# Layer 1's maxima turned one head at a time, in column order, and the softmax factors applied three steps later

## The chip, the cores and the metric

The kernel runs on one core of a Trainium2 chip. The metric is the device time of one execution in microseconds (us). Engines are named as the profile names them: PE multiplies matrices (PEld is its weight load), DVE is the vector engine, ACT the scalar engine, POOL the GpSimd engine, and SP issues most of the DMA. PE writes to PSUM, a memory of eight banks of 128 x 512 fp32 values; everything else lies in SBUF or in DRAM.

## The reference

Two attention layers follow each other on an image batch x of shape (2, 256, 64, 64), so 4096 positions for each of two batch elements. The first has heads of 16 channels and ends in a gated residual with a sigmoid. The change concerns the second:

```python
qkv = jnp.einsum('oc,bchw->bohw', w_qkv, x) + b_qkv[None, :, None, None]
qkv = qkv.reshape(b, HEADS, 3 * head_dim, h * w)          # 4 heads of 64
q, k, v = jnp.split(qkv, 3, axis=2)
attn = jax.nn.softmax(jnp.einsum('bhdn,bhdm->bhnm', q, k) * scale, axis=-1)
out = jnp.einsum('bhnm,bhdm->bhnd', attn, v).reshape(b, c, h, w)
return jnp.einsum('oc,bchw->bohw', w_out, out) + b_out[None, :, None, None] + x
```

Each row of the softmax runs over all 4096 keys. All of it is fp32.

## The kernel before, in words

Layer 1 is cut into 32 units (b, g, j): batch element, pair of heads, block of 512 queries. A unit goes over the 4096 keys in 32 chunks of 128. For one chunk, `score` (L847) makes the scores of both heads, 128 keys by 2 x 512 queries, in a PSUM tile of two banks called "pair", of which there are two. `keep` (L864) takes a running maximum of them on DVE (`rmax`, L875; the very first chunk of a unit needs none) and copies them to SBUF on ACT (`raw`, L876). The ring of raw tiles holds 26 chunks.

The softmax's maximum is taken in two groups of 16 chunks. When a group's scores are all made, `turn_max` (L882) transposes the running maxima with eight 128 x 128 transposes, both heads into one tile of the pair kind, so that keys lie along the free side; `fold` (L893) reduces them on DVE to one negated maximum for each query (L898), writes these to DRAM (`neg`, L902) and reads them back spread over all partitions (`row`, L904). `place_shift` (L917) copies that row to PSUM. Twenty-two chunks after its score, a chunk gets the row added on DVE (`shift`, L925), its exponential on ACT (`weigh`, L937), and is added to a sum over keys on POOL (`acc`, L947 and L949; the first chunk of a group needs no addition of its own). A chunk or two later `gather` multiplies it with the values (`av`, L959).

When all chunks of a unit are through, the totals over keys are made on PE (`total`, L989), copied (L997), written to DRAM by four small DMAs and read back with queries along the partitions (`sums`, L1001). `factors` (L1014) scales the first group's sums, adds the two groups' on POOL (L1019, L1020), takes the reciprocal on DVE (L1022) and one product on POOL (L1023). `turn_sums` (L1026) transposes the unit's output four times for each group into the one bank of the "misc" kind, `rows` (L1029) multiplies by the factor on DVE (L1033) and adds on POOL (L1040, L1044), and a DMA writes the attention rows to DRAM (L1050).

The order on each engine is written out by hand. The main loop goes in steps of two chunks, so a unit has 16 steps, and unit n+1's step 0 follows unit n's step 15; the shifts lag 11 steps behind the scores. A step issues, in this order: both scores, the exponential of the second chunk of the step before, "start" and "early" work, keep and shift and exponential of the first chunk, "early end" work, keep of the second chunk, two gathers, "late" and "late end" work, shift of the second chunk. The planned extra work hangs at such places by the calls of `at`. In steps as counted here, with a unit's own late work falling in the next unit: keys and values of a later pair of heads at steps 2, 3, 5 and 6, next queries at 10 and 11, a group's maxima at 0 and 8, the shift row at 3 and 11, totals at 12, factors at the start of 14, rows of both groups in step 14. All users of "misc" (keys, values, queries, totals, turned outputs, output projections) share its one bank. SP runs its DMAs in order, and one that has to wait keeps back those behind it.

At the end of the kernel, the output projection's first half is filled in between the last steps by a list of steps (`FILL`, `project_half` at L1167).

Of the kernel before, what the change touches and what calls it, by code (L numbers as in the profile page):

```python
# [26 lines left out]
def conv_attention_kernel(  # L27
# [19 lines left out]
    nc = tc.nc  # L47
    B, _, N = x.shape
    NJ = N // NB
    NM = N // P  # L50
    PB = NB // P
# [3 lines left out]
    small = ctx.enter_context(tc.tile_pool(name="small", bufs=2))  # L55
# [83 lines left out]
    ident = const.tile([P, P], F32, tag="ident", name="ident")  # L139
# [68 lines left out]
    seq = tc.keep_in_program_order  # L208
# [3 lines left out]
    def at(t, place, step):  # L212
        extras.setdefault((t, place), []).append(step)
# [19 lines left out]
    with own0:  # L233
# [322 lines left out]
        for n, u in enumerate(units0):  # L556
# [6 lines left out]
            if u == units0[-1]:  # L563
                t1 = t0 + NM + 9
# [5 lines left out]
            else:  # L570
                t1 = t0 + NM + 15
# [79 lines left out]
        def misc(name):  # L651
            return small_bank[0](name)
# [57 lines left out]
        for i in range(NJ):  # L710
            k = (0, 0, i)
            t1 = T0 + 2 + 2 * i
# [3 lines left out]
            t1 = T0 + 20 + 3 * i if i < PB else END0 + (2, 3, 4, 9)[i - PB]  # L716
# [42 lines left out]
    GS = NM // 2  # L759
    NG = NM // GS  # L760
    LAG = GS // 2 + 3
    US = NM // 2
    END = len(units) * US
# [3 lines left out]
    with (  # L767
# [11 lines left out]
        rts = {}  # L779
        outs = {}  # L780
        halves_of = {}
        kd, vd = (
# [8 lines left out]
        neg1 = {  # L791
            (u, n): dram.tile([2, NB], F32, tag=f"neg_{u}_{n}", name=f"neg_{u[0]}{u[1]}{u[2]}_{n}")
            for u in units for n in range(NG)
        }
        sum1 = {
            u: dram.tile([NG * 2, NB], F32, tag="sum_{}_{}_{}".format(*u), name=f"sum_{u}")
            for u in units
        }
# [76 lines left out]
                seq(nc.vector.tensor_tensor(rmax[u, n], ps, before, ALU.max))  # L875
            seq(nc.scalar.copy(raw, ps))  # L876

        def by_query(a, i):

            return a.rearrange("p (q i) -> p i q", i=PB)[:, i, :]  # L880

        def turn_max(u, n):  # L882

            b, g, j = u
            ps = psp.tile([P, 2, NB], F32, tag="pair", name=f"rt_{b}_{g}_{j}_{n}")
            for k in range(2):
                for i in range(PB):
                    seq(nc.tensor.transpose(  # L888
                        ps[:, k, bass.ts(i, P)], by_query(rmax[u, n][:, k, :], i), ident
                    ))  # L890
            rts[u] = ps

        def fold(u, n):  # L893


            b, g, j = u
            nm = small.tile([P, 2, PB], F32, tag="negs", bufs=2 * NG, name=f"negs_{b}_{g}_{j}_{n}")
            seq(nc.vector.tensor_reduce(  # L898
                nm, rts.pop(u).rearrange("p k (i m) -> p k i m", m=P), AX.X, ALU.max, negate=True,
            ))  # L900
            to = neg1[u, n]
            nc.sync.dma_start(out=to.rearrange("k (p i) -> p k i", i=PB), in_=nm)  # L902
            row = l1.tile([P, 2, NB], F32, tag="row", bufs=1, name=f"row_{b}_{g}_{j}_{n}")
            nc.sync.dma_start(  # L904
                out=row.rearrange("p k n -> p (k n)"),
                in_=to.rearrange("(o k) n -> o (k n)", o=1).partition_broadcast(P),
            )
            rows_in[u, n] = row
            negs[u, n] = nm
            if n == 1:  # L910

                lost = small.tile([P, 2, PB], F32, tag="lost", name=f"lost_{b}_{g}_{j}")
                seq(nc.gpsimd.tensor_tensor(lost, nm, negs.pop((u, 0)), ALU.subtract))
                negs.pop((u, 1))
                losts[u] = lost

        def place_shift(u, n):  # L917
            b, g, j = u
# [75 lines left out]
        def keep_total(u):  # L994
            b, g, j = u
            row = l1.tile([P, NB], F32, tag="kv", name=f"srow_{b}_{g}_{j}")
            seq(nc.scalar.copy(row, srows[u]))  # L997
            for m in range(2 * NG):
                nc.sync.dma_start(out=sum1[u][m : m + 1, :], in_=row[32 * m : 32 * m + 1, :])
            s = small.tile([P, NG, 2, PB], F32, tag="sums1", name=f"sums1_{b}_{g}_{j}")  # L1000
            nc.sync.dma_start(  # L1001
                out=s.rearrange("p n k i -> p (n k) i"),
                in_=sum1[u].rearrange("m (p i) -> p m i", i=PB),
            )
            srows[u] = s
            seq(nc.scalar.activation(losts[u], losts[u], AF.Exp, scale=D1**-0.5))

        def turned(a, name):
            ps = misc(name)
            for i in range(PB):  # L1010
                seq(nc.tensor.transpose(ps[:, bass.ts(i, P)], by_query(a, i), ident))  # L1011
            return ps.rearrange("p (i k d) -> p k i d", k=2, d=D1)

        def factors(u):  # L1014

            b, g, j = u
            s = srows.pop(u)
            lost = losts.pop(u)
            seq(nc.gpsimd.tensor_tensor(s[:, 0], s[:, 0], lost, ALU.mult))  # L1019
            seq(nc.gpsimd.tensor_tensor(s[:, 1], s[:, 1], s[:, 0], ALU.add))  # L1020
            f = small.tile([P, NG, 2, PB], F32, tag="f1", name=f"f1_{b}_{g}_{j}")
            seq(nc.vector.reciprocal(f[:, 1], s[:, 1]))  # L1022
            seq(nc.gpsimd.tensor_tensor(f[:, 0], f[:, 1], lost, ALU.mult))  # L1023
            joined[u] = f

        def turn_sums(u, n):  # L1026
            avs1[u, n] = turned(avs1[u, n], "turned_{}_{}_{}_{}".format(*u, n))

        def rows(u, n):  # L1029
            b, g, j = u  # L1030
            ps = avs1.pop((u, n))
            r = l1.tile([P, 2, PB, D1], F32, tag="rows", name=f"rows_{b}_{g}_{j}_{n}")
            seq(nc.vector.tensor_tensor(  # L1033
                r, ps, joined[u][:, n].unsqueeze(3).to_broadcast([P, 2, PB, D1]), ALU.mult
            ))
# [12 lines left out]
            for k in range(2):  # L1048
                queue = (nc.sync, nc.scalar)[k if last else 0]
                queue.dma_start(  # L1050
                    out=to[2 * g + k, bass.ts(j, NB), :].rearrange("(p i) d -> p i d", i=PB),
                    in_=r[:, k, :, :],
                )
                if last:
                    c = ((2 * g + k) * N + j * NB) // D1
                    queue.dma_start(
                        out=last_att[0][c % P : c % P + NB // D1, :],
                        in_=att[b][c : c + NB // D1, :],
                    )
# [29 lines left out]
        for n, u in enumerate(units):  # L1089
            b, g, j = u  # L1090
# [6 lines left out]
            if n < len(units) - NJ:  # L1097
                to = (*units[n + NJ][:2], j)
# [84 lines left out]
        for i in range(NJ - 3):  # L1183
# [96 lines left out]
```

## Time and profile before

| | |
|---|---|
| median of 3 executions | 4988.03 us (4970.19 to 4988.19) |
| the profiled execution | 4990.49 us, span of its profile 4988.7 us |
| PE busy over the span | 4573.0 us (92%) |
| DVE busy | 3908.3 us (78%) |
| ACT busy | 3427.6 us (69%) |
| POOL busy | 2499.0 us (50%) |
| layer 0, from the span's start to 2050 us | PE 2031.87, DVE 1440.72, ACT 1200.74, POOL 149.32 us busy |
| layer 1's main part, 2050 to 4900 us | PE 2478.00, DVE 2425.66, ACT 2203.70, POOL 2328.80 us busy |
| its end, 4900 to 4988.7 us | PE 63.11, DVE 41.92, ACT 23.17, POOL 20.88 us busy |

The two layers have different limits, so busy shares over the whole span say little. In layer 1 four engines work in a chain on two score tiles, and what a stage costs is read from its waits: the number in square brackets behind an instruction in the view by time is how long its engine stood idle before it, and what ended that.

### The profile page before, as it was taken

The page shows a single profiled execution, that of the slowest core. Times are in us where ns is not written, and L with a number is a line of the kernel's source. Part 1 is how long each engine was busy: PE and PEld are TensorE (multiplying, and loading weights), DVE is VectorE, ACT ScalarE, POOL GpSimd, SP SyncE. Part 2 cuts the span into 40 slices and gives each one's busy share as a digit, 9 for nine tenths or more (in the row PEclk, how much of TensorE's full clock was granted, in tenths as well). Part 3 has the DMA queues.
Part 4 walks back from the last instruction along what each step waited for, and adds up shares of the span by engine and source line. Part 5 has one row for each costly group of instructions (what it writes and reads, how often), then busy time and mean ns, then how long its engine had stood idle before and what let it go on. Part 6 is the DMA issues. An engine that isn't in the chain of part 4 may idle for free. (4 is left out here: it accounts for less than half of the span.)

```text
span 4988.7 us, 69799 instructions
## 1 busy us (share of the span) xinstructions
PE 4573.0 (92%) x26998; PEld 1533.3 (31%) x26998; DVE 3908.3 (78%) x4456; ACT 3427.6 (69%) x4508; POOL 2499.0 (50%) x1294
## 2 busy tenths in 40 slices
PE   8999999999999999888888888888889988888887
PEld 4433333333333333322222322222223222222222
DVE  6777777777777774488888888888888888888885
ACT  3366666666666666688777787878777777787773
POOL 5300000000000000188888888888877788888883
PEclk9999999999999999999999999999999999999998
DMA  3000000000000001211111110112112111000012
GB/s 98 32 6 18 18 18 14 23 14 14 14 16 14 14 12 46 68 31 38 30 37 52 49 33 30 37 30 64 43 55 69 59 47 55 24 20 24 22 32 77
DMA packets 132625, 174.65 MB, mean 35 GB/s; under 512 B 54584, under 2 KB 63608, under 8 KB 132164
## 3 DMA queue, kind: packets, MB, share of 16 engines
q1 hardware_dynamic: 130868, 169.59, 11.2%
q8 instruction: 212, 3.47, 0.3%
q14 instruction: 121, 0.99, 0.1%
q10 hardware_dynamic: 1424, 0.59, 0.1%
HBM read 127.66 MB, written 42.48 MB: 34 GB/s over the span
## 5 line engine op out<-in xcount | busy, mean ns | idle before, releaser
L949 POOL TENSOR_TENSOR acc<-acc,raw 128x1024 f32<-128x1024 f32 x883 | 2092.6, 2370 | 272.1 <-ACT raw L937 216.5
L402 DVE TENSOR_REDUCE mx<-a 128x1 f32<-128x512 f32 x2048 | 1315.3, 686 | 448.9 <-PE a L398 447.9
L439 ACT ACTIVATE p<-s 128x512 f32<-128x512 f32 x2048 | 1107.8, 595 | 702.1 <-PE a L398 369.3
L876 ACT COPY raw<-s 128x1024 f32<-128x1024 f32 x1024 | 1037.0, 1013 | 545.9 <-DVE rmax L875 451.8
L858 PE MATMUL s<-q,k 64*128 64x512 f32 x4096 | 1149.2, 654 | 192.2 <-ACT raw L876 188.5
L875 DVE TENSOR_TENSOR rmax<-s,rmax 128x1024 f32<-128x1024 f32 x960 | 1169.7, 1218 | 108.6 <-PE s L858 103.5
L925 DVE TENSOR_TENSOR raw<-raw,shift 128x1024 f32<-128x1024 f32 x1024 | 1236.5, 1211 | 20.3 <-ACT shift L920 19.5
L436 PE MATMUL s<-q,kT 32*128 32x512 f32 x4096 | 1217.8, 640 | 0.0
L937 ACT ACTIVATE raw<-raw 128x1024 f32<-128x1024 f32 x1024 | 1087.2, 1062 | 100.3 <-DVE raw L925 59.0
L398 PE MATMUL a<-kT,q 32*128 32x512 f32 x4096 | 1129.0, 643 | 1.4 <-DVE mx L402 1.3
L959 PE MATMUL av<-raw,v 128*64 128x512 f32 x4096 | 1021.8, 620 | 1.7 <-ACT avs L976 1.7
L451 PE MATMUL av<-p,v 128*32 128x256 f32 (+1 forms) x7904 | 650.1, 399 | 0.6 <-ACT avs L465 0.6
L858 PEld LDWEIGHTS s<-q,k 64*128 64x128 f32 x4096 | 333.0, 192 | 979.4 <-ACT raw L876 715.7
L436 PEld LDWEIGHTS s<-q,kT 32*128 32x128 f32 x4096 | 397.0, 183 | 425.9 <-issue 392.8
L501 POOL TENSOR_TENSOR f<-f,dyn 128x16 f32<-128x16 f32 x15 | 3.3, 221 | 1027.4 <-DVE f L500 1027.4
L959 PEld LDWEIGHTS av<-raw,v 128*64 128x64 f32 x4096 | 255.6, 140 | 627.5 <-issue 529.6
L451 PEld LDWEIGHTS av<-p,v 128*32 128x32 f32 x7904 | 157.6, 108 | 751.5 <-issue 737.3
L552 POOL TENSOR_SCALAR res<-res 128x1024 f32<-128x1024 f32 x16 | 16.7, 1045 | 660.0 <-ACT res L551 660.0
L398 PEld LDWEIGHTS a<-kT,q 32*128 32x128 f32 x4096 | 305.0, 183 | 31.5 <-DVE mx L402 18.2
L947 POOL TENSOR_TENSOR acc<-raw,raw 128x1024 f32<-128x1024 f32 x64 | 152.5, 2383 | 240.0 <-ACT raw L937 240.0
L898 DVE TENSOR_REDUCE negs<-rt 128x8 f32<-128x1024 f32 x64 | 78.4, 1224 | 131.5 <-PE rt L888 131.5
L1011 PE MATMUL turned<-ident,avs 128*128 128x128 f32 x256 | 59.6, 370 | 116.6 <-DVE rows L1033 116.6
(319 smaller groups left out, 1789.4 us busy)
## 6 DMA issues: line engine op xcount, KB each, us to landing
row<-neg SPq DMA_DIRECT2D x64, 512.0 KB
x<-in_x_dram SPq DMA_DIRECT2D x16, 512.0 KB
res<-in_x_dram SPq DMA_DIRECT2D x16, 512.0 KB
x<-res SPq DMA_DIRECT2D x16, 512.0 KB
att<-rows SPq DMA_DIRECT2D x63, 128.0 KB
kd<-k1s SPq DMA_DIRECT2D x24, 256.0 KB
vd<-v1s SPq DMA_DIRECT2D x24, 256.0 KB
k<-kd SPq DMA_DIRECT2D x24, 256.0 KB
```

The lines of the kernel that those rows point to most:

```text
L398: seq(nc.tensor.matmul(ps, qs0[u][r, bass.ts(i, P)], kTs[b][r, bass.ts(m, NB)], start=True, stop=True,))
L402: seq(nc.vector.tensor_reduce(mxs[u][:, i * H + h, m : m + 1], ps, AX.X, ALU.max))
L436: seq(nc.tensor.matmul(ps, kTs[b][r, bass.ts(m, P)], qs0[u][r, :], start=True, stop=True))
L439: seq(nc.scalar.activation(pt[:, k, :], ps, AF.Exp, scale=D0**-0.5))
L451: seq(nc.tensor.matmul(avs[u][32 * h : 32 * h + 32, cols], vs0[b][:, m, 32 * h : 32 * h + 32], pts[t, h // 2][:, h % 2, cols], start=(m == ...
L858: seq(nc.tensor.matmul(ps[:, k, :], ks[b, g, m // PB][r, bass.ts(m % PB, P)], qs1[u][r, :], start=True, stop=True,))
L875: seq(nc.vector.tensor_tensor(rmax[u, n], ps, before, ALU.max))
L876: seq(nc.scalar.copy(raw, ps))
L925: seq(nc.vector.tensor_tensor(raws[t], raws[t], shifts[u, t % NM // GS], ALU.add))
L937: seq(nc.scalar.activation(p, p, AF.Exp, scale=D1**-0.5))
L949: seq(nc.gpsimd.tensor_tensor(accs[u, n], accs[u, n], p, ALU.add))
L959: seq(nc.tensor.matmul(avs1[u, n][k * D1 : (k + 1) * D1, :], v[:, m % PB, k, :], raws[t][:, k, :], start=(m % GS == 0), stop=(m % GS == GS ...
```

## The change

It has four parts. First, `turn_max` and `fold` handle one head at a time: four transposes into the misc bank and a reduction of 512 elements, at the places "early" and "late" of the same step in which both heads were handled together; each head has its own DMA to DRAM and back. Second, the transposes take contiguous columns where they took every fourth (`by_query` is gone). With that, partition p holds queries p, p + 128, p + 256 and p + 384 in place of four neighbours, so the DMAs of maxima and sums move single fp32 values where they moved four, and the attention rows go out in pieces of 64 values where a partition wrote 256 in one piece. Third, the difference of the two groups' maxima (`lose`) gets its own place in step 9. Fourth, the two sums on POOL move from the start of step 14 to the end of step 13, the reciprocal and the product to the start of step 15, and the rows to step 17, which is step 1 of the unit after; the list of fills at the kernel's end moves with them.

```diff
-            ps = psp.tile([P, 2, NB], F32, tag="pair", name=f"rt_{b}_{g}_{j}_{n}")
-            for k in range(2):
-                for i in range(PB):
-                    seq(nc.tensor.transpose(
-                        ps[:, k, bass.ts(i, P)], by_query(rmax[u, n][:, k, :], i), ident
-                    ))
-            rts[u] = ps
+            ps = misc(f"rt_{b}_{g}_{j}_{n}_{k}")
+            for i in range(PB):
+                seq(nc.tensor.transpose(
+                    ps[:, bass.ts(i, P)], rmax[u, n][:, k, bass.ts(i, P)], ident
+                ))
+            rts[k] = ps
...
-                nm, rts.pop(u).rearrange("p k (i m) -> p k i m", m=P), AX.X, ALU.max, negate=True,
+                nm, rts[k].rearrange("p (i m) -> p i m", m=P), AX.X, ALU.max, negate=True
             ))
-            to = neg1[u, n]
-            nc.sync.dma_start(out=to.rearrange("k (p i) -> p k i", i=PB), in_=nm)
-            row = l1.tile([P, 2, NB], F32, tag="row", bufs=1, name=f"row_{b}_{g}_{j}_{n}")
-            nc.sync.dma_start(
-                out=row.rearrange("p k n -> p (k n)"),
-                in_=to.rearrange("(o k) n -> o (k n)", o=1).partition_broadcast(P),
-            )
+            nc.sync.dma_start(out=to.rearrange("o (i p) -> p (o i)", p=P), in_=nm)
+            nc.sync.dma_start(out=rows_in[u, n][:, k, :], in_=to.partition_broadcast(P))
+
+        def lose(u):
+
+            b, g, j = u
+            lost = small.tile([P, 2, PB], F32, tag="lost", name=f"lost_{b}_{g}_{j}")
+            seq(nc.gpsimd.tensor_tensor(lost, negs.pop((u, 1)), negs.pop((u, 0)), ALU.subtract))
+            losts[u] = lost
...
-                in_=sum1[u].rearrange("m (p i) -> p m i", i=PB),
+                in_=sum1[u].rearrange("m (i p) -> p m i", p=P),
...
-                seq(nc.tensor.transpose(ps[:, bass.ts(i, P)], by_query(a, i), ident))
+                seq(nc.tensor.transpose(ps[:, bass.ts(i, P)], a[:, bass.ts(i, P)], ident))
...
-        def factors(u):
-
-            b, g, j = u
-            s = srows.pop(u)
-            lost = losts.pop(u)
+        def add_sums(u):
+            s, lost = srows[u], losts[u]
             seq(nc.gpsimd.tensor_tensor(s[:, 0], s[:, 0], lost, ALU.mult))
             seq(nc.gpsimd.tensor_tensor(s[:, 1], s[:, 1], s[:, 0], ALU.add))
+
+        def factors(u):
+
+            b, g, j = u
             f = small.tile([P, NG, 2, PB], F32, tag="f1", name=f"f1_{b}_{g}_{j}")
-            seq(nc.vector.reciprocal(f[:, 1], s[:, 1]))
-            seq(nc.gpsimd.tensor_tensor(f[:, 0], f[:, 1], lost, ALU.mult))
+            seq(nc.vector.reciprocal(f[:, 1], srows.pop(u)[:, 1]))
+            seq(nc.gpsimd.tensor_tensor(f[:, 0], f[:, 1], losts.pop(u), ALU.mult))
             joined[u] = f
...
-                    out=to[2 * g + k, bass.ts(j, NB), :].rearrange("(p i) d -> p i d", i=PB),
+                    out=to[2 * g + k, bass.ts(j, NB), :].rearrange("(i q) d -> q i d", q=P),
...
-                at(t1, "early", lambda u=u, k=k: turn_max(u, k))
-                at(t1, "early end", lambda u=u, k=k: fold(u, k))
+                for i, place in enumerate(("early", "late")):
+                    at(t1, place, lambda u=u, k=k, i=i: turn_max(u, k, i))
+                    at(t1, f"{place} end", lambda u=u, k=k, i=i: fold(u, k, i))
...
-            at(t1 + 6, "start", lambda u=u: factors(u))
+            at(t1 + 1, "late", lambda u=u: lose(u))
+            at(t1 + 5, "late end", lambda u=u: add_sums(u))
+            at(t1 + 7, "start", lambda u=u: factors(u))
             for place, k in (("early", 1), ("late", 0)):
-                at(t1 + 6, place, lambda u=u, k=k: turn_sums(u, k))
-                at(t1 + 6, f"{place} end", lambda u=u, k=k: rows(u, k))
+                at(t1 + 9, place, lambda u=u, k=k: turn_sums(u, k))
+                at(t1 + 9, f"{place} end", lambda u=u, k=k: rows(u, k))
...
-            (END + GS // 2 + 4, "early end"): (3,), (END + GS // 2 + 5, "early"): (4,),
-            (END + GS // 2 + 5, "early end"): (5,), (END + GS // 2 + 6, "early end"): (6, 7),
+            (END + GS // 2 + 4, "early end"): (3, 4), (END + GS // 2 + 9, "early end"): (5,),
+            (END + GS // 2 + 9, "late end"): (6, 7),
```

More of the change, by code (lines that the diff above doesn't have):

```diff
@@ L778, in conv_attention_kernel @@
         avs1, srows, losts, joined, halves = {}, {}, {}, {}, {}
-        rts = {}
+        rts = [None, None]
         outs = {}
@@ L876, in keep, with turn_max @@
             seq(nc.scalar.copy(raw, ps))
-        def by_query(a, i):
-            return a.rearrange("p (q i) -> p i q", i=PB)[:, i, :]
-        def turn_max(u, n):
+        def turn_max(u, n, k):
             b, g, j = u
-            ps = psp.tile([P, 2, NB], F32, tag="pair", name=f"rt_{b}_{g}_{j}_{n}")
-            for k in range(2):
-                for i in range(PB):
-                    seq(nc.tensor.transpose(
-                        ps[:, k, bass.ts(i, P)], by_query(rmax[u, n][:, k, :], i), ident
-                    ))
-            rts[u] = ps
@@ L893, in fold @@
-        def fold(u, n):
-            b, g, j = u
-            nm = small.tile([P, 2, PB], F32, tag="negs", bufs=2 * NG, name=f"negs_{b}_{g}_{j}_{n}")
+            ps = misc(f"rt_{b}_{g}_{j}_{n}_{k}")
[4 more added lines that the diff above has]
+            rts[k] = ps
+        def fold(u, n, k):
+            b, g, j = u
+            if k == 0:
+                negs[u, n] = small.tile(
+                    [P, 2, PB], F32, tag="negs", bufs=2 * NG, name=f"negs_{b}_{g}_{j}_{n}"
+                )
+                rows_in[u, n] = l1.tile(
+                    [P, 2, NB], F32, tag="row", bufs=1, name=f"row_{b}_{g}_{j}_{n}"
+                )
+            nm, to = negs[u, n][:, k, :], neg1[u, n][k : k + 1, :]
@@ L908, in fold @@
[L908 to L915, printed above, removed]
+            nc.sync.dma_start(out=to.rearrange("o (i p) -> p (o i)", p=P), in_=nm)
+            nc.sync.dma_start(out=rows_in[u, n][:, k, :], in_=to.partition_broadcast(P))
@@ L1010, in turned @@
             for i in range(PB):
-                seq(nc.tensor.transpose(ps[:, bass.ts(i, P)], by_query(a, i), ident))
+                seq(nc.tensor.transpose(ps[:, bass.ts(i, P)], a[:, bass.ts(i, P)], ident))
             return ps.rearrange("p (i k d) -> p k i d", k=2, d=D1)
+        def add_sums(u):
+            s, lost = srows[u], losts[u]
+            seq(nc.gpsimd.tensor_tensor(s[:, 0], s[:, 0], lost, ALU.mult))
+            seq(nc.gpsimd.tensor_tensor(s[:, 1], s[:, 1], s[:, 0], ALU.add))
         def factors(u):
             b, g, j = u
-            s = srows.pop(u)
-            lost = losts.pop(u)
-            seq(nc.gpsimd.tensor_tensor(s[:, 0], s[:, 0], lost, ALU.mult))
-            seq(nc.gpsimd.tensor_tensor(s[:, 1], s[:, 1], s[:, 0], ALU.add))
             f = small.tile([P, NG, 2, PB], F32, tag="f1", name=f"f1_{b}_{g}_{j}")
-            seq(nc.vector.reciprocal(f[:, 1], s[:, 1]))
-            seq(nc.gpsimd.tensor_tensor(f[:, 0], f[:, 1], lost, ALU.mult))
+            seq(nc.vector.reciprocal(f[:, 1], srows.pop(u)[:, 1]))
+            seq(nc.gpsimd.tensor_tensor(f[:, 0], f[:, 1], losts.pop(u), ALU.mult))
             joined[u] = f
```

## The prediction, made before the changed kernel was run

> **What bounds the kernel now.** I read the page first, then busy time by stage, then the sums of waits over the second layer, then one unit in order of time, then the DMA of two short stretches.
>
> Busy time by stage (columns: stretch and its length, then PE, PEld, DVE, ACT and POOL busy with instruction counts, PE clock, DMA share, GB/s):
>
> ```profile
> 0.00:2050.00 2050.00, 2031.87 (x16969) 708.55 (x16970) 1440.72 (x2229) 1200.74 (x2186) 149.32 (x153) 0.99 0.08 24
> 3009.95:3098.69 88.74, 77.57 (x312) 25.46 (x313) 76.06 (x68) 69.67 (x74) 74.38 (x37) 0.96 0.11 34
> ```
>
> The first 2050 us are layer 0, which the diff leaves alone. The second line is one layer 1 unit, from its step 0 to the next unit's: 88.74 us, of which PE works 77.6, DVE 76.1, POOL 74.4. Three engines are nearly full and none is full: the 11 to 14 us missing on each are waits of one engine for another. The waits between 2110 and 4900 us (total, times, longest) name them:
>
> ```profile
> ACT raw L876 <- DVE rmax L875: 437.5, 247, 4.7
> PE s L858 <- ACT raw L876: 179.0, 303, 1.5
> DVE f L1022 <- POOL sums L1020: 134.5, 31, 4.4
> DVE negs L898 <- PE rt L888: 129.1, 62, 2.9
> PE turned L1011 <- DVE rows L1033: 115.4, 31, 3.8
> DVE rmax L875 <- PE s L858: 96.6, 162, 1.0
> ```
>
> DVE stands still for the reciprocal once a unit (134.5/31 = 4.3 us), for the turned maxima twice (129.1/62 = 2.1 us on average), and 3.1 us for scores. One unit's places, in order of time:
>
> ```profile
> 3081.39 1.13 PE L858 MATMUL s<-q,k 64*128 64x512 f32 x4 [0.90 <-ACT raw L876]
> 3082.45 0.75 PE L1011 MATMUL turned<-ident,avs 128*128 128x128 f32 x4
> 3085.24 0.20 POOL L1019 TENSOR_TENSOR sums<-sums,lost 128x8 f32<-128x8 f32 x1
> 3085.76 0.20 DVE L1022 RECIPROCAL f<-sums 128x8 f32<-128x8 f32 x1 [4.40 <-POOL sums L1020]
> 3088.85 1.13 PE L1011 MATMUL turned<-ident,avs 128*128 128x128 f32 x4 [3.79 <-DVE rows L1033]
> 3094.30 1.22 DVE L875 TENSOR_TENSOR rmax<-s,rmax 128x1024 f32<-128x1024 f32 x1
> 3098.69 1.98 PE L888 MATMUL rt<-ident,rmax 128*128 128x128 f32 x8 [0.89 <-ACT raw L876]
> 3100.71 1.22 DVE L898 TENSOR_REDUCE negs<-rt 128x8 f32<-128x1024 f32 x1 [2.93 <-PE rt L888]
> 3108.91 1.22 DVE L875 TENSOR_TENSOR rmax<-s,rmax 128x1024 f32<-128x1024 f32 x1
> ```
>
> At step 14 POOL reaches the sums only at 3085.24, since the addition of chunk 5 stands before them, and that waits for ACT's exponential of the chunk that DVE shifted last. The reciprocal, next on DVE, waits 4.40 us for it; score copies, PE's second turn (3.79) and everything else wait behind it. The DMA of the maxima (first) and of the sums (second), over 2.4 and 4.0 us:
>
> ```profile
> DMA packets 272, 0.00 MB, mean 2 GB/s; under 512 B 272, under 2 KB 272, under 8 KB 272
> q1 hardware_dynamic: 272, 0.00, 6.2%
> ...
> DMA packets 528, 0.01 MB, mean 2 GB/s; under 512 B 528, under 2 KB 528, under 8 KB 528
> q1 hardware_dynamic: 528, 0.01, 7.0%
> ```
>
> 6.2% of 16 engines over 2.4 us is 2.38 us for 272 packets; 7.0% of 4.0 us is 4.48 us for 528: 8.5 to 8.8 ns a packet of 16 bytes.
>
> **What the Trainium skill says.** "DMA: Bandwidth & Descriptors", Rules for kernel authors: a strided last dimension "Lowers to one descriptor per element". The trace agrees in kind: 256 runs of 16 bytes give 256 packets, plus 16. Its Specifications say that below 512 B a DMA does read-modify-write; the 16-byte writes are below that already, and the next DMA is issued 1.6 to 3.0 us after theirs. "TensorE: Matmul & The Clock Gate", Part 1: a PE that idles is throttled. The trace agrees: eight transposes took 1.98 us at 3098.69, behind the stall, and 1.24 at 3051.89.
>
> **The change, part by part.** Instructions pass on DVE every 1.13 us when nothing waits (starts 3059.96, 3061.09, 3062.23).
>
> *Reciprocal to step 15, rows to step 1.* Before, DVE needs 12.94 us from the end of chunk 5's shift (3081.36) to the last maximum (3094.30): the 4.40 us wait, six passes, two rows of about 0.65, small gaps. After, the sums stand on POOL behind chunk 4's addition, and the reciprocal on DVE behind chunk 7's shift, so DVE has six passes and 0.2: 7.0 us. Gain 5.9. The cover: chunk 5's shift ends three passes before chunk 7's, chunk 4's addition is through by about 3082.8 + 0.6 for the sums, and the reciprocal comes at 3086: 2.5 us to spare. Beyond that, each us that the sums are late is a us of DVE. The scores of step 15 follow in time, since PE needs 1.13 + 0.97 a chunk against DVE's 2.26.
>
> *The DMAs of the sums.* 512 pieces of 16 bytes become 2048 of 4. By engine time 128 x 8.5 = 1.1 us an engine instead of 0.3; by the 0.6 us that the packets lay apart, 2.3. I take +1.7. The read was issued at 3077.54 and its like in the tail landed within 2.0 us; 3081.2 is still ahead of POOL's arrival. Bounds: 0, and as in the slower rival.
>
> *Maxima, step 8.* Before, the fold ran 3053.17 to 3054.39 after a 1.30 us wait, and the next group's second maximum came at 3056.57. After, four transposes (half of 1.24, up to the 0.75 of the turn; I take 0.7) follow the scores at 3050.75 at once, and the first fold starts when DVE is free, 3051.86. A fold of 512 elements: layer 0's reduction of 512 is 686 ns against 1224 for 1024, so some 0.62 in a row. Fold, maximum to 3053.65; PE: gather 1.94, second turn to 3053.9 or so; wait 0.3, fold, shift; the maximum of 3056.57 comes at 3055.75. Gain 0.8. Second turn needs the bank that the first fold frees at 3052.5, a us before PE asks.
>
> *Maxima and rows, steps 0 and 1.* Before, 3094.30 to 3108.91 = 14.6 us. After, nine passes of 1.13, two folds of 0.62 and two rows of 0.65 = 12.7. Waits: the step's second score can't start before 3096.67 (ACT's copy), ends 3097.80, first turn 3098.5, DVE free at 3097.75: 0.8. Gather to 3100.45, second turn 3101.15, DVE free at 3100.3: 0.85. Sum 14.4. The two turns of rows: first behind two scores, second ready 0.3 us ahead of DVE. Gain 0 to 0.3; I take 0. Bounds -1.6 (both waits vanish) and +2.
>
> *Maxima's DMAs.* Two writes of 512 pieces of 4 bytes and two broadcasts of 256 KB for one of each: SP issues 4 instead of 2, some 0.35 us each, which nobody waits for. On SP the first broadcast waits for the first write, and at step 0 the second write stands behind it. First fold at +4.6 from step 0, write to issue of the next DMA 2.3 by the median of the same pair now, twice, and 3.3 for a half broadcast (the whole one's packets end about 4.0 after its issue): lands at +12.9. ACT wants it at step 3, +19.8 (3025.77 against 3005.91): 6.9 us to spare, 5.5 at step 8. Hidden.
>
> *The rest.* POOL: same instructions; 30 additions at 2.43, rows 2.6, small ones 0.9: 76.3 a unit. By the shifts above it lags at most 2.8 us (chunk 10's), repaid at the next group's first chunk, which needs no addition; a ring buffer comes back four chunks later. The attention rows go out in 256-byte pieces instead of 1 KB, 0.5 us longer, read units later. Cost 0. Tail: the sums' DMA +1.7, one fill instead of two before the last rows -1.3, row pieces +0.5: +1.
>
> Sum: 31 x 5.9 + 32 x 0.8 = 209 us, less 1. The profiled execution took 4990.5 (span 4988.7), giving 4782; it stands 2.5 above the median 4988.0, so 4780. A unit would take 82.0 us, with PE at about 77.
>
> **Rivals.** *The one bank eats part (0.20).* PE, DVE and PE hand over in turn at steps 0, 1 and 8; if each costs a us more than replayed, or POOL, then at 93% of a unit, passes its 2.8 us lag on through ring or totals: some 3 x 31 = 93 us less, 4873. For it: PE and DVE are both within 6 us of 82. Against it: DVE, not PE, comes last in all but two hand-overs above.
>
> *Slower: single elements are dear (0.13).* Place: the sums' read before POOL's L1019. Chunk 4's addition covers it until 3084.5 or so; with 1.6 us fixed and 128 elements an engine that is 42 ns an element. At about 95 ns the 6.7 us of gain are gone; above, the kernel is slower, and POOL's additions queue behind. At 150 ns the stall is 14 us a unit: 31 x 7 more than now, some 5205. Against it: 8.5 ns a packet. For it: no 4-byte scatter of this size runs now.
>
> *No change (0.04).* The reciprocal's wait only moves to step 15, since POOL runs later without the stall: 4988.
>
> *The forecast (0.63)*, own range 4740 to 4825: both waits of step 0 gone, or 1.4 us a unit lost.
>
> **The numbers.** 0.5% is 25 us, what a measurement of this kernel can tell from no change. Faster: 0.63 + 0.20 = 0.83; same 0.04; slower 0.13. The range 4730 to 4885 takes in the forecast and most of the first rival.
>
> **What would show it.** Right: no wait of DVE f for POOL sums worth a us; folds of about 0.69 waiting under 1 us; units of 82 us; PE's transposes about 0.7 for four. Wrong: L1012 waiting for DMA sums (dear elements); shift copies on ACT waiting for row; PE's second turn waiting for the first fold or for rows; the exponentials waiting for POOL, or PE's totals for acc.

## The result, and the profile after

The changed kernel takes 5207.8 us (median of 4 runs, 5201.26 to 5213.43) against 4985.35 for the kernel before on the same chip: a ratio of 1.0452, 95% interval 1.0427 to 1.0478. It is 222 us slower; the forecast was 205 us faster. The profiled execution took 5201.26 us, its span 5199.4.

Layer 0 is what it was (PE busy 2030.33 us up to 2050, before 2031.87). Busy time by stage, with the columns of the prediction's first view; the lines are layer 1's main part and one of its units, here from one issue of the sums' read to the next:

```profile
2050.00:5100.00 3050.00, 2497.95 (x9827) 763.36 (x9827) 2423.04 (x2239) 2209.76 (x2298) 2319.01 (x1126) 0.93 0.17 38
2967.25:3063.31 96.06, 79.11 (x318) 24.22 (x314) 76.76 (x71) 69.86 (x73) 73.64 (x36) 0.93 0.14 31
```

A unit of 88.7 us has become one of 96 (the next takes 92.96), and DVE and POOL work no longer for it than before: DVE 76.8 us (76.1 before), POOL 73.6 (74.4). PE's 79.1 (77.6 before) go with a lower granted clock, 0.93 where it was 0.96. So the time is again in waits. Between 2110 and 5100 us they are (total, times, longest):

```profile
PE s L858 <- ACT raw L876: 520.2, 340, 10.4
DVE raw L921 <- ACT shift L916: 393.0, 62, 12.2
ACT shift L916 <- DMA row<-neg: 357.9, 62, 11.4
ACT raw L876 <- DVE rmax L875: 228.8, 267, 4.6
DVE rmax L875 <- PE s L858: 133.4, 160, 3.6
DVE negs L900 <- PE rt L883: 48.0, 94, 0.7
```

The reciprocal's wait (134.5 us before) is gone, and the folds wait 48 us where they waited 129. In their place stands a chain whose first link the profile before lacks: ACT's copy of the shift row waits for the DMA that brings the row, 62 times, 5.8 us each on average; DVE's shift waits for ACT (17.4 us in all before); PE's scores wait for the score tile that ACT, held up, has not copied.

One such place in order of time, from the folds of step 0 to the shift of step 3 (start, duration, engine or queue, idle time before it and what ended that):

```profile
2982.93 0.69 DVE L900 TENSOR_REDUCE negs<-rt 128x4 f32<-128x512 f32 x1 [0.65 <-PE rt L883]
2983.65 0.38 SPq L903 DMA_DIRECT2D neg<-negs  x1
2985.39 0.69 DVE L900 TENSOR_REDUCE negs<-rt 128x4 f32<-128x512 f32 x1 [0.64 <-PE rt L883]
2992.00 0.34 SPq L904 DMA_DIRECT2D row<-neg  x1
2992.43 0.39 SPq L903 DMA_DIRECT2D neg<-negs  x1
3003.24 0.34 SPq L904 DMA_DIRECT2D row<-neg  x1
3008.16 1.02 ACT L916 COPY shift<-row 128x1024 f32<-128x1024 f32 x1 [9.61 <-DMA row<-neg]
3009.21 1.22 DVE L921 TENSOR_TENSOR raw<-raw,shift 128x1024 f32<-128x1024 f32 x1 [10.16 <-ACT shift L916]
3010.17 2.08 PE L858 MATMUL s<-q,k 64*128 64x512 f32 x4 [8.62 <-ACT raw L876]
```

The first head's maxima leave at 2983.65. The broadcast that has to wait for this write is issued at 2992.00, 8.35 us later. Before, the same pair lay 2.33 us apart (1.55 to 3.25 over all 64 pairs, median 2.2):

```profile
3013.22 0.37 SPq L902 DMA_DIRECT2D neg<-negs  x1
3015.55 0.32 SPq L904 DMA_DIRECT2D row<-neg  x1
```

The second head's maxima are ready at 2986.1, but their write stands behind that broadcast on SP and goes out at 2992.43; its own broadcast follows 10.81 us later. ACT has been ready for the row since 2998.55 and gets it at 3008.16. Behind such a stall PE is slower as well: the four score matmuls at 3010.17 take 2.08 us at a granted clock of 0.50, where they took 1.13 at 2992.66 at a clock of 1.00.

The DMA engines themselves are not busy in these gaps. Their view between the first write and the next DMA (busy tenths in 40 slices of 0.21 us, then packets, then the queue's share of 16 engines):

```profile
DMA  0000281000000000000000000000000000000000
...
DMA packets 528, 0.00 MB, mean 0 GB/s; under 512 B 528, under 2 KB 528, under 8 KB 528
...
q1 hardware_dynamic: 528, 0.00, 3.0%
```

All 528 packets lie in three slices, some 0.8 to 1.4 us after the issue; 3.0% of 16 engines over 8.4 us is 4.03 us, 7.6 ns a packet, no more than a 16-byte packet cost before. The remaining 6.9 us hold no packet. SP isn't busy either: at step 8 it issues the second write while the first is still open. What is late is the write's completion, that is, the moment from which a DMA that depends on the write may be issued.

At step 8 the queue holds both writes ahead of both broadcasts (writes from 3037.18, broadcasts at 3045.34 and 3049.3), so two late completions overlap, and ACT waits 2.08 us there where it waits 9.61 at step 0.

DVE, which does every chunk's maximum and shift, gives the account best. The waits of DVE alone, in us over layer 1's main part of each kernel; the last four columns belong to experiments told below:

| DVE waits for | before | after | by query | factors later alone | one head alone | one broadcast |
|---|---|---|---|---|---|---|
| sums on POOL (reciprocal) | 134.5 | none | none | none | 134.8 | none |
| PE's turned maxima (fold) | 129.1 | 48.0 | 58.9 | 110.3 | 60.4 | 47.4 |
| PE's scores (maximum) | 96.6 | 133.4 | 69.2 | 69.8 | 85.7 | 134.9 |
| ACT's shift row (shift) | 17.4 | 393.0 | 26.5 | 29.2 | 15.5 | 170.5 |
| kernel, median us | 4985 | 5208 | 4753 | 4819 | 4908 | 4955 |

### The profile page after: what moved, and what is told of

Read it like the earlier page. It is cut to its first block, busy times and chain, and to the rows that moved or that the text cites. A ratio compares the mean times of both kernels' runs of the same rounds, so it can differ in the third digit from the quotient of the medians.

```text
span 5199.4 us, 70140 instructions
## 1 busy us (share of the span) xinstructions
PE 4593.8 (88%) x26998; PEld 1491.6 (29%) x26998; DVE 3907.9 (75%) x4520; ACT 3434.6 (66%) x4508; POOL 2491.9 (48%) x1294
## 5 line engine op out<-in xcount | busy, mean ns | idle before, releaser
L858 PE MATMUL s<-q,k 64*128 64x512 f32 x4096 | 1182.0, 669 | 536.3 <-ACT raw L876 532.9
L955 PE MATMUL av<-raw,v 128*64 128x512 f32 x4096 | 1036.2, 627 | 10.1 <-ACT avs L972 10.1
L916 ACT COPY shift<-row 128x1024 f32<-128x1024 f32 x64 | 65.1, 1016 | 371.6 <-DMA row<-neg 371.6
L900 DVE TENSOR_REDUCE negs<-rt 128x4 f32<-128x512 f32 x128 | 88.3, 690 | 50.7 <-PE rt L883 50.6
```

Of the source, the lines that this page charges most:

```text
L858: seq(nc.tensor.matmul(ps[:, k, :], ks[b, g, m // PB][r, bass.ts(m % PB, P)], qs1[u][r, :], start=True, stop=True,))
L955: seq(nc.tensor.matmul(avs1[u, n][k * D1 : (k + 1) * D1, :], v[:, m % PB, k, :], raws[t][:, k, :], start=(m % GS == 0), stop=(m % GS == GS ...
```

## The experiments

**The changed kernel by query again.** If the 4-byte pieces are the cause, everything else of the change should do what was forecast. The column order is undone everywhere, so that a partition holds four neighbouring queries again and writes them as one piece of 16 bytes; the rest is kept:

```diff
-                    ps[:, bass.ts(i, P)], rmax[u, n][:, k, bass.ts(i, P)], ident
+                    ps[:, bass.ts(i, P)], by_query(rmax[u, n][:, k, :], i), ident
...
-            nc.sync.dma_start(out=to.rearrange("o (i p) -> p (o i)", p=P), in_=nm)
+            nc.sync.dma_start(out=to.rearrange("o (p i) -> p (o i)", i=PB), in_=nm)
```

and likewise in the sums' read, in `turned` and in the DMA of the rows.

> The changed kernel with only the column order undone: maxima, sums, outputs and attention rows by query again, so 16-byte pieces and 1 KB rows; one head at a time, the one bank and the later factors stay. Theory (writes of single elements to DRAM are confirmed late, and the shift row with them): 4750 to 4830 us, no wait of ACT shift for DMA row, no wait of the reciprocal. Rival (hand-overs through the one bank or POOL cost the time): stays at 5150 to 5210.

Measured: 4753.24 us (4751.01 to 4757.39), ratio to before 0.9541 (0.9527 to 0.9556). It is the fastest of all, 455 us below the changed kernel. Its busy time by stage, and its waits between 2110 and 4650 us:

```profile
2050.00:4660.00 2610.00, 2394.39 (x9813) 761.89 (x9813) 2418.32 (x2236) 2201.73 (x2297) 2324.22 (x1126) 1.00 0.17 44
```

```profile
PE s L858 <- ACT raw L876: 185.9, 301, 1.7
ACT raw L876 <- DVE rmax L875: 161.1, 238, 1.8
DVE rmax L875 <- PE s L858: 69.2, 109, 0.9
DVE negs L904 <- PE rt L887: 58.9, 93, 0.8
DVE raw L925 <- ACT shift L920: 26.5, 48, 0.9
```

ACT no longer waits for the row at all. The clock is 1.00, and PE needs 104 us less for the same work. Against the changed kernel DVE waits 366.5 us less for the shift row and 64.2 less for scores, 10.9 more for the folds: 420 of the 455 us. The scores' 64 us fit the clock: PE's score matmuls are busy 1152.4 us in the changed kernel's main part and 1083.5 here. The edit also changes the order in which PE's transposes read their columns. That isn't what cost the time: the maxima's transposes take 82.7 us in the changed kernel and 93.1 here. At step 0 its queue has the same order as the changed kernel's:

```profile
3014.78 0.35 SPq L907 DMA_DIRECT2D neg<-negs  x1
3017.25 0.33 SPq L908 DMA_DIRECT2D row<-neg  x1
3017.68 0.38 SPq L907 DMA_DIRECT2D neg<-negs  x1
3020.68 0.32 SPq L908 DMA_DIRECT2D row<-neg  x1
```

Two gaps of 2.5 and 3.0 us where the changed kernel has 8.35 and 10.81.

**Column order alone in the kernel before.** The same lines the other way round: `by_query` is taken out of the kernel before, which keeps both heads together and the factors at step 14.

```diff
-            nc.sync.dma_start(out=to.rearrange("k (p i) -> p k i", i=PB), in_=nm)
+            nc.sync.dma_start(out=to.rearrange("k (i p) -> p k i", p=P), in_=nm)
```

> The kernel before with only the column order of the change: both heads at once as before, factors at step 14 as before. Theory of late writes: one write of 1024 single elements is confirmed some 8 us after its issue instead of 2.3, slack was about 6, so 2 to 3 us lost twice a unit: 5080 to 5200 us, ACT shift waits for DMA row. Rival (bank and schedule cost the time): 4980 to 5000, no such wait.

Measured: 5143.54 us (5130.47 to 5146.76), ratio 1.0319 (1.03 to 1.0337). There is a loss without any of the rest. Its waits between 2110 and 5000 us:

```profile
DVE raw L925 <- ACT shift L920: 132.7, 59, 3.3
DVE f L1022 <- POOL sums L1020: 128.4, 30, 4.4
ACT shift L920 <- DMA row<-neg: 114.0, 61, 2.6
DVE negs L898 <- PE rt L888: 110.4, 62, 3.1
```

With one write for both heads (1024 pieces) there is one late completion to a group, 8.6 to 11.3 us between write and broadcast over the 64 pairs, and the row is late by 1.9 us on average. The loss is 159 us, 5.1 a unit. In the changed kernel two such completions stand in a row at step 0.

**Column order for sums and rows, maxima by query.** Which of the three transfers is it? The changed kernel with the maxima alone by query; the sums' read of 2048 single values and the rows' pieces of 256 bytes stay. The maxima's differences then meet other queries' sums, which changes values and no instruction.

```diff
-                    ps[:, bass.ts(i, P)], rmax[u, n][:, k, bass.ts(i, P)], ident
+                    ps[:, bass.ts(i, P)], by_query(rmax[u, n][:, k, :], i), ident
...
-            nc.sync.dma_start(out=to.rearrange("o (i p) -> p (o i)", p=P), in_=nm)
+            nc.sync.dma_start(out=to.rearrange("o (p i) -> p (o i)", i=PB), in_=nm)
```

> The changed kernel with the maxima alone by query (16-byte writes); sums, outputs and attention rows stay in column order. The factor of the group maxima's difference is paired with the wrong queries, so one factor of the softmax is left wrong; all work is done. Theory (the maxima's writes alone): within 1% of the run with everything by query, 4750 to 4830 us. Rival (the 2048-element read of the sums, or the 256-byte attention rows, matter too): well above it, up to 5000.

Measured: 4754.41 us (4751.97 to 4757.49), ratio 0.9544 (0.9529 to 0.956): the same as by query throughout. The read of single values and the short row pieces cost nothing that can be measured. Of the column order only the maxima's writes count.

**The price of a small write by itself.** A kernel of small writes alone, each followed by a read that depends on it, so that the gap between their issues is the time until the write counts as done. It was executed once; eleven rounds of each shape could be read.

```python
nc.sync.dma_start(out=to[0:1, :].rearrange("o (i p) -> p (o i)", p=P), in_=src[:, 0, :])   # cols
nc.sync.dma_start(out=to[0:1, :].rearrange("o (p i) -> p (o i)", i=PB), in_=wide[:, :, 0]) # near
nc.sync.dma_start(out=to[:, 0].rearrange("(i p) -> p i", p=P), in_=src[:, 0, :])           # apart
```

> Leaves both layers out: it copies x to the output and then, one after the other and nothing beside, writes small tiles to DRAM in eight shapes, each followed by a read of it that has to wait for the write; then reads 2048 values back in column order and by query. Gap from a write's issue to the read's issue. Theory (single elements land late because several pieces of one line are written apart): both heads by query and one head by query 1.5 to 2 us, columns 7 to 9 us, single elements next to each other as slow as columns or between, elements 64 or 512 bytes apart fast (2 us) if it is the sharing of a line and slow (8 us) if it is the size alone; one 2 KB line 1.5. Rival (the number of packets): all shapes of 512 packets alike at 2 us, and the time is lost in the kernel by traffic beside it. Reads: columns at most 2 us longer than by query.

Gap from the write's issue to the read's:

| write | pieces | us, lowest to highest | median |
|---|---|---|---|
| both heads by query | 256 x 16 B | 1.56 to 2.86 | 2.3 |
| one head by query | 128 x 16 B | 1.43 to 3.02 | 1.5 |
| one head in column order (cols) | 512 x 4 B, packed | 8.25 to 11.14 | 8.8 |
| the same, a partition's four side by side (near) | 512 x 4 B, packed | 6.77 to 8.60 | 7.1 |
| one value for each partition (single) | 128 x 4 B, packed | 7.20 to 9.27 | 7.5 |
| each value in its own 64 B (apart) | 512 x 4 B | 1.85 to 2.73 | 1.9 |
| each value in its own 512 B (far) | 512 x 4 B | 1.77 to 2.00 | 1.8 |
| one line | 1 x 2 KB | 1.16 to 1.57 | 1.2 |

One round of it on SP (start, duration, line):

```profile
118.50 0.35 SPq L89 DMA_DIRECT2D single<-src  x1
126.31 0.21 SPq L102 DMA_DIRECT2D got_single<-single  x1
...
140.64 0.38 SPq L68 DMA_DIRECT2D cols<-src  x1
148.89 0.21 SPq L102 DMA_DIRECT2D got_cols<-cols  x1
...
162.41 0.38 SPq L78 DMA_DIRECT2D apart<-src  x1
164.26 0.21 SPq L102 DMA_DIRECT2D got_apart<-apart  x1
```

It isn't the number of pieces: 128 packed single values are nearly as late as 512. It isn't their size either: 512 single values that lie apart take 1.9 us. The DMA engines show the same for both: 528 packets of 7.7 to 7.8 ns, the last of them some 1.3 us after the issue, at 140.64 as at 162.41; the read follows 7 us behind that last packet in the one case and 0.6 in the other. Single values that lie packed side by side in DRAM are what is dear. Reading 2048 values in column order takes 3.4 us to the next issue against 2.3 by query (medians): reads lack the effect.

**The two parts alone.** The gain of the version by query has two sources, and the prediction priced each. First the kernel before with the factors later:

```diff
-            at(t1 + 6, "start", lambda u=u: factors(u))
+            at(t1 + 5, "late end", lambda u=u: add_sums(u))
+            at(t1 + 7, "start", lambda u=u: factors(u))
...
-                at(t1 + 6, place, lambda u=u, k=k: turn_sums(u, k))
-                at(t1 + 6, f"{place} end", lambda u=u, k=k: rows(u, k))
+                at(t1 + 9, place, lambda u=u, k=k: turn_sums(u, k))
+                at(t1 + 9, f"{place} end", lambda u=u, k=k: rows(u, k))
```

> The kernel before with one part of the change alone: the two sums on POOL at the end of step 13, reciprocal and product at step 15, rows in step 17 (and the fills at the kernel's end with them). Maxima stay with both heads at once in a pair tile, by query, in 16-byte pieces. The prediction's sum gives this part 31 x 5.9 = 183 us: 4985 - 183 = some 4800, with no wait of f for POOL sums. Rival A, that the gain of the version by query (231 us) comes from the maxima turned one head at a time: 4930 to 4985 here. Rival B, that the eight transposes at step 0, now just behind no rows at all and ahead of two turns of rows in step 1, stall more than before: 4840 to 4880.

Measured: 4818.94 us (4816.45 to 4822.18), ratio 0.9672 (0.9654 to 0.969), 167 us faster. Then one head at a time, by query, with the factors left at step 14:

```diff
-                at(t1, "early", lambda u=u, k=k: turn_max(u, k))
-                at(t1, "early end", lambda u=u, k=k: fold(u, k))
+                for i, place in enumerate(("early", "late")):
+                    at(t1, place, lambda u=u, k=k, i=i: turn_max(u, k, i))
+                    at(t1, f"{place} end", lambda u=u, k=k, i=i: fold(u, k, i))
```

> The kernel before with the other part alone: maxima turned one head at a time in the misc bank, by query, with two writes of 16-byte pieces and two broadcasts, and the difference of the maxima in a place of its own; sums, factors and rows stay at step 14. The prediction's sum gives it 32 x 0.8 = 26 us: some 4960, with the wait of negs for PE's turn under 1 us each and the reciprocal's wait for POOL still about 4.3 us a unit. Rival A: it brings most of the 231 us, 4760 to 4850. Rival B: the one bank, which rows in step 14 use as well, eats it: 4985 to 5030. If both parts simply add up, the gains of this run and of the late factors alone make 231 us.

Measured: 4907.54 us (4906.24 to 4910.2), ratio 0.9851 (0.9829 to 0.9872), 78 us faster, three times what was expected. 167 + 78 = 245, and together, in the version by query, they bring 231: the parts nearly add up.

Both expectations divided the sum wrongly. The two rows on DVE, 1.3 us a unit, leave step 14 in the prediction's first term and arrive in its second (steps 0 and 1), so the one is 1.3 too high and the other 1.3 too low. Booked in their places, factors later give 31 x (5.9 - 1.3) = 143 us, and one head at a time 31 x (0.2 + 1.3) + 32 x 0.8 = 72. The second agrees with 78, and the place agrees too: in the table the folds' wait falls by 69 us and that for scores by 11. The first is short by 24 us. The table says where more was gained: beside the reciprocal's 134.5 us DVE waits 18.8 us less for the folds and 26.8 less for scores, and 11.8 more for the shift row. The folds' part lies in PE's transposes of the maxima. The kernel before (its next step 0, at 3098.69, stands in the prediction):

```profile
3009.95 1.98 PE L888 MATMUL rt<-ident,rmax 128*128 128x128 f32 x8 [0.89 <-ACT raw L876]
```

and with the factors later alone:

```profile
3039.63 1.24 PE L888 MATMUL rt<-ident,rmax 128*128 128x128 f32 x8 [0.89 <-ACT raw L876]
```

The granted clock over these lines is 0.50 in the first and 1.00 in the second. Summed over the main part the maxima's transposes take 98.8 us before and 80.0 with the factors later: 18.8 less, as much as the folds' wait. That the stall of step 14 lowers the clock fits these two places, and is not shown: in six units of the kernel before step 0 takes 1.24 us behind the same stall, and in its last eight step 8 takes 1.70 to 1.84 without one.

**One broadcast behind both writes.** If the late completions cost by standing in series, then putting them side by side must give much of the time back, with the 4-byte writes unchanged. In the changed kernel, both heads' row is read by one broadcast after the second write:

```diff
-            nc.sync.dma_start(out=rows_in[u, n][:, k, :], in_=to.partition_broadcast(P))
+            if k == 1:
+                nc.sync.dma_start(
+                    out=rows_in[u, n].rearrange("p k n -> p (k n)"),
+                    in_=neg1[u, n].rearrange("(o k) n -> o (k n)", o=1).partition_broadcast(P),
+                )
```

> The changed kernel, column order and 4-byte writes kept, with one broadcast of both heads behind both writes in place of a broadcast behind each. At step 0 the changed kernel issues write, broadcast, write, broadcast on SP, so that the second write (2992.43) is issued only when the first is confirmed (8.4 us), though its maxima were ready at 2986.08; at step 8 it issues both writes first, and there the row is late by 2.1 us where it is late by 9.6 us at step 0. Theory (late confirmations, in series on SP): here the second write goes at +2.5 us behind the first, the broadcast some 10 us later, the row lands some 2 us late at both steps, and 7.5 us a unit come back, with what hangs on them: 65% of the 455 us that lie between the changed kernel and the version by query, so some 4910 (4850 to 4970). Rival, that the 4-byte writes slow the engines by something else than the wait for the row (traffic, the memory, the order of columns on PE): the time stays within 5150 to 5210.

Measured: 4955.3 us (4952.32 to 4962.98), ratio 0.9947 (0.9927 to 0.9967). 252 of the 455 us are back, 55% where 65% was expected, inside the range given. One step 0:

```profile
3008.43 2.81 SPq L903 DMA_DIRECT2D neg<-negs  x2
3019.28 0.34 SPq L905 DMA_DIRECT2D row<-neg  x1
...
3025.32 1.02 ACT L920 COPY shift<-row 128x1024 f32<-128x1024 f32 x1 [2.00 <-DMA row<-neg]
```

The row is late by 2.0 us here and by 2.65 at the step 8 before it. Against the version by query DVE waits 144 us more for the shift row and 66 more for scores, 12 less for folds: 198 of the 202 us that are left. The wait for the row carries most of what is left, and the writes show no other harm; the wait for scores goes at least in part with PE's lower clock (0.976 over this profile, 0.995 by query).

**How densely must single values lie?** 512 pieces each time, spacing and size varied (the lines in the expectation are off: they are 55, 60, 65, 70, 75, 80 and 85 in the same order).

```python
to = dram.tile([M, 2], F32)                                                # step: 1, 2, 4, 8 or 16 values
nc.sync.dma_start(out=to[:, 0].rearrange("(i p) -> p i", p=P), in_=src[:, :4])
```

> Leaves both layers out and copies x to the output; then 10 rounds of seven small writes to DRAM, each followed by a read that waits for it. All are 512 pieces with neighbours on different partitions: single values 4, 8, 16, 32 and 64 bytes apart (lines 62, 67, 72, 77 and 82), and packed pieces of 8 and of 16 bytes (lines 87 and 92). Theory (the pieces that fall into one stretch of 64 bytes are written one after the other): 16 to a stretch took 7.1 to 8.8 us from the write's issue to the read's, one to a stretch 1.9, so some 1.4 + 0.45 us a piece in the stretch. That gives 8.6 us at 4 bytes apart, 5.0 at 8, 3.2 at 16, 2.3 at 32, 1.9 at 64; the packed pieces go by their number in a stretch too: 5.0 for 8 bytes, 3.2 for 16. Rival: a single value is slow as soon as it has any neighbour close by, whatever the number (8 at every spacing under 64), and pieces of 8 bytes and more are fast (under 2.6).

| 512 pieces | to a stretch of 64 B | expected us | measured, median | lowest to highest |
|---|---|---|---|---|
| 4 B, 4 B apart | 16 | 8.6 | 8.3 | 8.15 to 10.71 |
| 4 B, 8 B apart | 8 | 5.0 | 4.0 | 3.03 to 4.29 |
| 4 B, 16 B apart | 4 | 3.2 | 2.7 | 2.56 to 2.99 |
| 4 B, 32 B apart | 2 | 2.3 | 2.0 | 1.86 to 2.13 |
| 4 B, 64 B apart | 1 | 1.9 | 1.9 | 1.83 to 2.08 |
| 8 B, packed | 8 | 5.0 | 4.1 | 3.03 to 4.49 |
| 16 B, packed | 4 | 3.2 | 2.7 | 2.47 to 2.86 |

Medians are over 8 or 9 of the 10 rounds, those that ran clear of the copy of x. One round (the profile leaves the number out of the names, so L55 is the packed write, L60 8 bytes apart, L80 packed pieces of 8 bytes):

```profile
141.27 0.36 SPq L55 DMA_DIRECT2D step<-src  x1
149.60 0.24 SPq L92 DMA_DIRECT2D got_step<-step  x1
152.57 0.36 SPq L60 DMA_DIRECT2D step<-src  x1
156.61 0.24 SPq L92 DMA_DIRECT2D got_step<-step  x1
...
169.04 0.36 SPq L80 DMA_DIRECT2D eight<-src  x1
173.23 0.24 SPq L92 DMA_DIRECT2D got_eight<-eight  x1
```

The density of pieces decides and not their size: 4.0 and 4.1 us for eight to 64 bytes, 2.7 and 2.7 for four. The rival, that any close neighbour makes a single value slow, is out. The expected line is not met: from 8 to 16 pieces the time doubles. That 64 bytes is the stretch within which pieces hinder one another, and that they are written one after the other in it, are readings of these numbers and not shown by them. In all of these writes neighbours come from different partitions; whether that matters was tried only at the densest spacing (7.1 us for four side by side from one partition, 8.8 otherwise).

## Why the prediction was wrong

*Factors later: right.* No wait of the reciprocal for POOL is left in the main part; POOL was through with the sums in time (2973.83 in the changed kernel, the reciprocal at 2976.48: 2.65 us to spare, 2.5 forecast). Measured by itself 167 us, where the prediction has 183 for this part and 143 with the rows booked in their place.

*Maxima one head at a time: right, though booked 46 us too low.* Folds take 690 ns; the next instruction on DVE starts 0.61 us after a fold's start (0.62 was forecast). They wait 0.65 and 0.64 us at step 0 (0.8 and 0.85 forecast). The single bank holds PE up by some 0.4 us a unit (12.1 us in all), between the two turns of rows. Measured by itself 78 us, where the prediction has 26 for this part and 72 with the rows booked in their place.

*The sums' DMAs: right.* In the kernel of small transfers the read of column order costs 1.1 us more, forecast 1.7, and in this one it is covered.

*The rest: right.* POOL did not become the bound, and the 256-byte rows cost nothing. With the maxima's writes put right, the kernel takes 4753 us where the forecast says 4780, a unit 81.2 to 81.6 us where it says 82.0, PE 75.3 where it says 77. The forecast doesn't count on a higher clock, and the clock is 1.00; how much of the 27 us this makes up wasn't measured.

*"Maxima's DMAs ... Hidden": wrong, and this decides the sign.* This is the step of the prediction that failed. The chain itself was laid out as it came: write, broadcast, and the second write held behind the broadcast on SP. The term was mis-sized. "Write to issue of the next DMA 2.3 by the median of the same pair now, twice" measured 8.35 and 10.81, 14.6 us more than the 4.6 forecast; the half broadcast took 4.9 us from its issue to ACT's copy where 3.3 was forecast (the DMA of the attention rows goes out 0.4 us behind it, at 3003.63, and shares the DMA engines with it). These 16 us used up the 6.9 to spare and left the 9.6 us of stall, near enough. The 2.3 us came from a write of 16-byte pieces, and the prediction carries it over to 4-byte pieces with no reason at this place; the nearest to one is its remark that 16-byte writes are below the 512 B that it quotes already. What it prices by piece, for the sums, is engine time, and that is the wrong quantity here: the packets did stay at 7.6 ns each, while the completion, of which the profile before could say nothing for packed single values, went from 2.3 to 8 us and more. The prediction bounded the unknown price of single elements for the sums' read and not for this write, although the write is waited for twice in series.

The Trainium skill points to that quantity, though for another path. "DMA: Bandwidth & Descriptors", Anatomy of one DMA, is about DMAs that GpSimd issues, where these are issued by SP; it says that most of the fixed part of such a DMA is the wait for the target memory's receipt of the write, heaviest when that is HBM (the chip's DRAM). This trace shows a time at that place, since the packets are over by 1.4 us after the issue and the next DMA comes at 8.35; that it is the receipt, no run here shows. The same table gives the fixed part as about 2.0 us that scales with nothing. For SP's writes the measurement differs, 1.2 us for one line and 8.8 for 512 packed single values, and it decides.

*The rivals.* "Slower: single elements are dear" named 5205 us, and 5208 came, but this is coincidence. It put the stall on the sums' read ahead of POOL's addition, by a price of 150 ns for each element. A packet of the sums' read takes 8.6 ns in the changed kernel, reads lack the effect, and the stall stands on ACT's shift copy, behind the maxima's writes. "The one bank eats part" is refuted by the folds' waits, "no change" by the reciprocal's. Of the signs listed for a wrong forecast, "shift copies on ACT waiting for row" is the one that appeared.

## What to carry to other kernels

When a change makes the pieces of a small DMA write smaller, don't price it by its packets: look at the gap from the write's issue to the first thing that waits for it, and count how many such gaps stand in a row on the queue. A write of single values into packed DRAM with a read waiting for it is better given as pieces of 16 bytes, or the values spread out; if it can't be avoided, issue all such writes before the first dependent read, so that they complete side by side. And test a change in parts: without the column order this change was worth 231 us, and the column order cost 455 (159 in the kernel before, where one late completion stands in a group and not two in a row).

## What the runs showed of the hardware

A DMA write to DRAM of 512 single fp32 values lets a DMA that depends on it be issued 8.3 to 8.8 us after its own issue when they lie packed (medians), 7.1 when four neighbours come from one partition, and 7.5 with only 128 of them; at 8, 16, 32 and 64 bytes apart it is 4.0, 2.7, 2.0 and 1.9 us. Packed pieces of 8 and 16 bytes behave as single values of the same spacing. Where it was looked up, the DMA engines show its last packet 1.3 us after the issue, packed or spread out alike (1.6 for the four neighbours from one partition). Reading 2048 values in the packed layout costs 1.1 us more than reading them in 16-byte pieces. A write and its read-back, twice in a row on one queue, add their completions (the row comes 7.8 to 11.4 us late at step 0); with both writes ahead of the reads they overlap (0.4 to 3.4 us late behind the first group). Behind a wait of 8.6 us PE's granted clock was 0.50, and four matmuls took 2.08 us in place of 1.13.
